# A recurrent block with a mixture of experts: rows split and loaded in another order, the gate's copies on ScalarE, states in a lasting PSUM bank, final sums and reciprocals queued a step later

## The chip, the cores and the metric

The kernel runs on one core of one Trainium2 chip. The metric is the device time of one execution in microseconds (us); several runs give a median. A profile is one execution recorded by the hardware. In it PE is TensorE (PEld its weight loads), DVE is VectorE, ACT is ScalarE, POOL is GpSimd and SP is SyncE, which here issues most of the DMAs. Each engine works through its own queue in order; an instruction that waits holds up all that stand behind it on that engine.

## The reference

There are 8 sequences of 512 tokens with 512 features, 16 heads of 32, and 16 experts of which each token takes 4. All is float32.

```
xn = layernorm(x)                                  # per token, no weights
q, k = rotate(silu(xn @ Wq)), rotate(silu(xn @ Wk)); v = xn @ Wv
o  = lightning_attention(q, k, v)                  # chunks of 128 tokens, a state of 32x32 per head
     # o_chunk = (q k^T * D) v + (q * decay_q) S ;  S = lam^128 * S + (k * decay_k)^T v
o  = o * sigmoid(xn @ Wg1 @ Wg2)                   # the gate
o  = o / sqrt(mean of squares per head + eps) * norm_weight
s  = o @ Wo
p  = softmax(xn @ gate_w.T); top 4, renormed
mixed  = sum over the 4 of p_e * (silu(xn @ Wg[e]) * (xn @ Wu[e])) @ Wd[e]
shared = (silu(xn @ sWg) * (xn @ sWu)) @ sWd * sigmoid(xn @ shared_gate_w)
out = x + s * silu(mixed + shared)
```

## The kernel before

The program has three stages.

The first stage (0 to about 340 us) normalises all eight sequences, routes their tokens, computes the shared expert, and runs the attention of sequences 0 and 1 among it. `norm(b)` makes statistics (DVE, L245 and L247), 1/std (POOL, L249 and L251) and centred rows (DVE, L237) in place in the tile `x_b`; there are three `x` buffers. `halves(b)` splits the low and the high halves of the second 256 features with four POOL copies (L266) and stores them in `xn_d`, from which the experts' rows are gathered later. `turn(b)` transposes the rows on PE (L285) and copies them out on ACT (L287). `load_x(b)` (L147) issues the next rows on SP. `route_1`, `route_2`, `share_1` and `share_2` do the router and the shared expert. The generator `first()` yields these pieces in order, and `along()` inserts them between the pieces of attention: nine fifths of a piece at each step. At the end of the stage, `sort()` and `table()` work out for each of 143 blocks of 128 rows which tokens it holds, with large DVE operations and PE matmuls (L517) in between.

The second stage (about 350 to 785 us) is the 143 expert blocks, each a gather, transposes, two matrix products and a scaled store to `y_d`.

The third stage (about 790 us to the end) runs the attention of sequences 2 to 7 (`sequence`, and `last_sequence` for 7), about 75 us each, with the mixture and the output of all tokens among it. `mixture(b, t)` loads the shared part into `m` (12 buffers), gathers four rows per token on POOL (L1107), adds them on POOL (L1113, L1116) and DVE (L1118, L1121) and applies Silu on ACT (L1124). It is a generator: each call of `advance()` (the `step` of a sequence) takes every active mixture a piece further. `last` multiplies by `s` (DVE, L1135), adds `x` (POOL, L1142, into `xo` with 4 buffers) and stores the result (L1143).

Order on the engines: PE's matmuls are fixed in program order by `on_pe()`. `behind(engine)` does the same for single instructions of POOL, DVE and ACT: they are queued behind the last one traced. All others are placed by a scheduler that may move them within its limits. A PSUM tile comes from `bank(tag, name)`: tag `a` has four banks, `k` and `m` one each, `d` two.

The gate of sequence b: `gate_1` makes `xn @ Wg1` in four row groups (PE, L568) and copies it to SBUF (DVE, L572, tile `g1`); `gate_2` adds the four groups with one matmul (PE, L577, `pf`) and copies that too (DVE, L579, tile `g2`); `gate_3` multiplies by Wg2 (PE, L588, `p`) and takes the sigmoid on ACT (L591, `on`).

The states: `by_token(b, g)` transposes three chunks of keys into bank `k` (PE, L622, `pk`) and scales them out (DVE, L625, `kd`). `scores` then writes the chunks' key-value products into the last 128 columns of the same bank (PE, L640), scores into four `a` banks (PE, L651), and DVE runs the recurrence over the products (L654 and L656, `state`) and masks the scores (L667). `output` adds both parts (PE, L679 and L685). `squares(b)` squares on ACT (L696), sums on PE (L699), takes the root on ACT (L703) and the reciprocal on DVE (L704); `normed(b)` spreads it and multiplies. `project` is the product with Wo (PE, L726).

Of the kernel before, what the change touches and what calls it, by code (L numbers as in the profile page):

```python
# [16 lines left out]
ALU = mybir.AluOpType  # L17
# [77 lines left out]
def tile_block(ctx: ExitStack, tc: tile.TileContext, a: dict, out: bass.AP):  # L95
# [8 lines left out]
    def bank(tag, name):  # L104
        return pp.tile([P, 512], F32, tag=tag, name=name, bufs={"a": 4, "k": 1, "m": 1, "d": 2}[tag])
# [155 lines left out]
    def halves(b):  # L261
        xs = xs_of[b]
        for t in range(NC):
            hs = p1.tile([P, D], U16, tag="hs", name=f"hs_{b}_{t}", bufs=4)
            with behind(POOL):
                nc.gpsimd.tensor_copy(  # L266
                    hs.rearrange("p (h d) -> p h d", h=2),
                    xs[:, t, D // 2 :].bitcast(U16).rearrange("p (d h) -> p h d", h=2))
            g = b * NC + t
            nc.sync.dma_start(xn_d[g * P : (g + 1) * P, D : 2 * D], hs)  # L270
        xs_of.pop(b)

    def turn(b):

# [271 lines left out]

    between = [lambda: None]

    def value(b, t):
        if t == 0:  # L550
            v_of[b] = att.tile([P, NC, D], F32, tag="v", name=f"v_{b}", bufs=2)
        pv = bank("d" if t % 2 else "m", f"pv_{b}_{t}")
        for k in range(KC):
            with on_pe():
                nc.tensor.matmul(  # L555
                    pv, lhsT=xT_of[b][:, k, t * P : (t + 1) * P], rhs=wv[:, k, :],
                    start=(k == 0), stop=(k == KC - 1))
            between[0]()
        nc.scalar.copy(v_of[b][:, t, :], pv)
# [4 lines left out]
    def gate_1(b):  # L564
        pg1 = bank("a", f"pg1_{b}")
        with on_pe():
            for k in range(KC):
                nc.tensor.matmul(  # L568
                    pg1[k * Q : (k + 1) * Q, :], lhsT=wg1[:, k, :], rhs=xT_of[b][:, k, :],
                    start=True, stop=True)  # L570
        g1_of[b] = att.tile([P, N], F32, tag="tmp", name=f"g1_{b}", bufs=TMP)
        nc.vector.tensor_copy(g1_of[b], pg1)  # L572

    def gate_2(b):
        pf = bank("a", f"pf_{b}")
        with on_pe():
            nc.tensor.matmul(pf, lhsT=four, rhs=g1_of[b], start=True, stop=True)  # L577
        g1_of[b] = att.tile([P, N], F32, tag="tmp", name=f"g2_{b}", bufs=TMP)
        nc.vector.tensor_copy(g1_of[b], pf)  # L579

    def gate_3(b):
        on_of[b] = home(b).tile([P, G, N], F32, tag="on", name=f"on_{b}", bufs=1)
# [33 lines left out]

    def by_token(b, g):

        pk = bank("k", f"pk_{b}_{g}")
        with on_pe():  # L620
            for c in range(NC - 1):
                nc.tensor.transpose(  # L622
                    pk[:, c * P : (c + 1) * P], kT_of[g][:, c * C : (c + 1) * C], ident)
        kd = scr[0].tile([P, NC - 1, HG, HD], F32, tag="kd", name=f"kd_{b}_{g}")
        nc.vector.tensor_tensor(  # L625
            kd, pk[:, : (NC - 1) * P].rearrange("p (c h d) -> p c h d", c=NC - 1, d=HD),
            dk[:, g * HG : (g + 1) * HG].unsqueeze(1).unsqueeze(3).to_broadcast(
                [P, NC - 1, HG, HD]), ALU.mult)
        kd_of[g] = pk[:, (NC - 1) * P :], kd
# [62 lines left out]
    def squares(b):  # L692
        pr = bank("a", f"pr_{b}")
        for g in range(G):
            sq = scr[0].tile([P, N], F32, tag="sc", name=f"sq_{b}_{g}", bufs=4)
            nc.scalar.activation(sq, on_of[b][:, g, :], AF.Square)  # L696
            with on_pe():
                for c in range(NC):
                    nc.tensor.matmul(  # L699
                        pr[c * Q : (c + 1) * Q, :C], lhsT=sel[:, H - HG - g * HG :][:, :Q],  # L700
                        rhs=sq[:, c * C : (c + 1) * C], start=(g == 0), stop=(g == G - 1))
        rs = att.tile([P, C], F32, tag="tmp", name=f"rs_{b}", bufs=TMP)
        nc.scalar.activation(rs, pr[:, :C], AF.Sqrt, bias=eps_rms, scale=1.0)  # L703
        nc.vector.reciprocal(rs, rs)  # L704
        rs_of[b] = rs

    def normed(b):
        pbs = [bank("a", f"pb_{b}_{c}") for c in range(NC)]
# [34 lines left out]
    def sequence(b, step, projected, before=None, defer=False, also=lambda: None):  # L743


        n = b + 1

        def project_tiles(q, ts):
            if q is not None:
                for t in ts:  # L750
                    projected(q, t, project(q, t))


        fill = ([0], [1], [2], [3], [], [], [], [])
        for g in range(G):
            scores(b, g)
            step()
            if g + 2 < G:
                key(b, g + 2)
            else:  # L760
                value(n, 2 * (g - 2))
            if g == 0 and b not in on_of:
                gate_3(b)
            if g + 1 < G:
                by_token(b, g + 1)
            project_tiles(before, fill[2 * g])
            step()
            if g + 2 < G:
                query(b, g + 2)
                if g + 3 == G and n not in xT_of:  # L770
                    load_xT(n)
            elif defer:
                (gate_1, gate_2)[g - 2](n)
            if g + 2 == G:
                value(n, 1)
            project_tiles(before, fill[2 * g + 1])
            if fill[2 * g + 1] == [NC - 1]:
                on_of.pop(before, None)
            output(b, g)
            step()  # L780
        v_of.pop(b)
        if n == FIRST:
            gate_1(n)
            squares(b)
            value(n, 3)
            normed(b)
            gate_2(n)
            return
        if defer:
            gate_3(n)  # L790
        value(n, 3)
        also()
        squares(b)
        step()
        key(n, 0)
        also()
        query(n, 0)
        normed(b)
        also()
        step()  # L800
        key(n, 1)
        by_token(n, 0)
        query(n, 1)
        also()
        if not defer:
            for gate, half in ((gate_1, [0, 1]), (gate_2, [2, 3])):
                gate(n)
                project_tiles(b, half)
                also()
            on_of.pop(b)  # L810
        step()

    def last_sequence(b, step, projected, before):
# [44 lines left out]
        for g in range(G):  # L858
            scores(b, g)
            step()  # L860
            if g + 2 < G:
                key(b, g + 2)
            if g > 1:
                project_before(2 * g - 3)
            if g:
                squares_of(g - 1)
            if g + 1 < G:
                by_token(b, g + 1)
            step()
            if g + 2 < G:  # L870
                query(b, g + 2)
            if g in (1, 2):
                project_before(2 * g - 2)
                normed_of(g - 1)
            output(b, g)
            step()
        add_up(0, (0, 1))
        normed_of(G - 2)
        add_up(1, (0, 1))
# [19 lines left out]
    def first():  # L899

        for b in range(B):
            route_1(b)
            yield
            share_1(b)
            yield
            if b + 2 < B:
                norm(b + 2)
            halves(b)
            if b + 3 < B:
                load_x(b + 3)  # L910
            if b + 1 < B:
                turn(b + 1)
                yield
            route_2(b)
            yield
            share_2(b)
            yield
        next(sorting)
# [2 lines left out]
    norm(0)  # L921
    turn(0)
    norm(1)
    pieces = first()
    for _ in range(5):
        next(pieces)
# [120 lines left out]
    def down(i):  # L1047
# [13 lines left out]
            y, py, row(i).bitcast(F32)[:, bass.ds(at, 1)], None, ALU.mult).ins)  # L1061
        nc.sync.dma_start(y_d[i * P : (i + 1) * P, :], y)


    for i in range(4):
        gather(i)
# [64 lines left out]
    def last(b, t, m, s):  # L1131
        xo = comb.tile([P, D], F32, tag="xo", name=f"xo_{b}_{t}", bufs=4)
        nc.sync.dma_start(xo, x[b, t * P : (t + 1) * P, :])
        with behind(DVE):
            nc.vector.tensor_tensor(m, m, s, ALU.mult)  # L1135

        if b + 1 == B and t % 2:
            with behind(DVE):
                nc.vector.tensor_tensor(xo, xo, m, ALU.add)  # L1139
        else:  # L1140
            with behind(POOL):
                nc.gpsimd.tensor_tensor(xo, xo, m, ALU.add)  # L1142
        nc.sync.dma_start(out[b, t * P : (t + 1) * P, :], xo)  # L1143


    m_of, active, steps = {}, [], [0, 0]
    waiting = [(q, t) for q in range(FIRST) for t in range(NC)]
    tiles = []
    for b in range(FIRST, B):
# [4 lines left out]
    def advance():  # L1154

        if steps[1] < len(tiles) and steps[0] * 5 >= steps[1] * 11:
            active.append(mixture(*tiles[steps[1]]))
            steps[1] += 1
        steps[0] += 1
        order = active[:]  # L1160
        while order:
            f = order.pop(0)
# [12 lines left out]
    for b in range(FIRST, B):  # L1175
# [2 lines left out]
            sequence(b, advance, finish, b - 1 if b > FIRST else None, True)  # L1178
        else:
            last_sequence(b, advance, finish, b - 1)  # L1180
    while active or steps[1] < len(tiles):
        advance()
    right.close()
    left.close()
# [53 lines left out]
```

## Time and profile before

| what | value |
|---|---|
| runs | 1246.65, 1247.88, 1249.57 us (median 1247.88) |
| the profiled execution's own time | 1250.12 us |
| its span | 1248.4 us, so 1.7 us lie outside the span |
| PE busy | 1188.4 us, 7799 matmuls and transposes |
| DVE busy | 772.1 us |
| ACT busy | 399.7 us |
| POOL busy | 448.9 us |
| mean granted clock of TensorE | 0.979 |

Busy time is the time in which an engine executes; what is left of the span is idle. The row `PEclk` of the page gives the clock granted to TensorE in tenths of full speed over 40 slices of the span. In a list of waits each line names an engine, the tile and line that waited, what released it, then the sum in us, how many times, and the longest. In a timeline each line has start, duration, engine, line, operation, what it writes and reads, and in brackets the idle time before it and what ended it. A row of the windows view has the window, its length, busy time and count by engine, the granted clock, the DMA share and GB/s.

### The profile page before, as it was taken

The numbers are of one execution on the slowest core, as the hardware profiler recorded it, in microseconds if no ns is written. First come the engines' busy times: TensorE is split into PE (matmuls) and PEld (weight loads), VectorE is DVE, ScalarE is ACT, GpSimd is POOL, SyncE is SP. The second block draws the span as 40 slices with busy tenths as digits, with TensorE's granted clock in tenths as the row PEclk, the third lists the DMA queues.
The fourth block names the chain that finished last, engine by engine and source line by source line (L and its number), as shares of the span: only waits on it lengthen the run. The fifth ranks groups of instructions, "written<-read, shape, count | busy, mean of one in ns | idle before, by whom it ended". The sixth has DMA issues, their size and how long they took to land. (4 is left out here: it accounts for less than half of the span.)

```text
span 1248.4 us, 21569 instructions
## 1 busy us (share of the span) xinstructions
PE 1188.4 (95%) x7799; PEld 703.8 (56%) x7799; DVE 772.1 (62%) x1668; ACT 399.7 (32%) x766; POOL 448.9 (36%) x430
## 2 busy tenths in 40 slices
PE   6988999988989999999999999999999999989997
PEld 3444554445557777777777777444544544445453
DVE  6458745699514444444444344887949879598784
ACT  3333334320144444444444443123141231411420
POOL 2112300300113333333333332580875857858311
PEclk9979899999989999999999999999989999999999
DMA  9676321162248999999999998950844636535112
GB/s 318 212 244 212 144 102 69 42 261 111 100 144 220 229 227 230 221 231 229 226 226 225 227 230 201 320 161 2 287 135 139 224 95 207 175 119 151 43 35 68
DMA packets 167719, 219.77 MB, mean 176 GB/s; under 512 B 93696, under 2 KB 102656, under 8 KB 165696
## 3 DMA queue, kind: packets, MB, share of 16 engines
q1 hardware_dynamic: 145936, 146.17, 40.0%
q0 software_dynamic: 21680, 72.23, 20.9%
q8 instruction: 64, 1.05, 0.3%
q14 instruction: 39, 0.32, 0.1%
HBM read 127.25 MB, written 72.35 MB: 160 GB/s over the span
## 5 line engine op out<-in xcount | busy, mean ns | idle before, releaser
L1030 PE MATMUL pgu<-wexp,xt 128*128 x1144 | 271.7, 381 | 0.7 <-ACT xt L1011 0.4
L1030 PEld LDWEIGHTS pgu<-wexp,xt 128*128 128x128 f32 x1144 | 217.4, 191 | 92.6 <-issue 32.1
L989 POOL DMA_INDIRECT xg<-xn_d,slot x83 | 78.4, 945 | 287.6 <-DVE y L1060 172.0
L1035 DVE TENSOR_TENSOR slb<-slb,pgu 128x128 f32<-128x128 f32 x143 | 41.2, 288 | 205.8 <-ACT slb L1034 205.8
L1013 ACT COPY xt<-pl 128x512 uint16<-128x512 uint16 x143 | 109.6, 767 | 156.3 <-DMA pl<-xg 92.3
L1107 POOL DMA_INDIRECT yg<-y_d,posi x128 | 141.9, 1108 | 49.5 <-DMA m<-sh_d 22.1
L1051 PE MATMUL py<-wexp,hT 128*128 x286 | 147.3, 597 | 0.0
L555 PE MATMUL pv<-wv,xT 128*128 128x512 f32 x256 | 121.3, 612 | 4.9 <-DVE sh L371 3.7
L597 PE MATMUL pk<-xT,wk 128*128 128x512 f32 x256 | 122.9, 621 | 0.0
L597 PE MATMUL pq<-xT,wq 128*128 128x512 f32 x256 | 115.9, 593 | 0.0
L726 PE MATMUL pw<-wo,on 128*128 128x512 f32 x224 | 102.6, 605 | 7.1 <-DVE m L1135 4.2
L1142 POOL TENSOR_TENSOR xo<-xo,m 128x512 f32<-128x512 f32 x30 | 44.6, 1488 | 153.3 <-DVE m L1135 149.3
L989 POOL DMA_INDIRECT more<-xn_d,slot x60 | 56.4, 941 | 114.4 <-DVE y L1060 113.5
L555 PEld LDWEIGHTS pv<-wv,xT 128*128 128x128 f32 x256 | 46.7, 194 | 62.4 <-issue 55.5
L1060 DVE TENSOR_SCALAR y<-py,xg 128x512 f32<-128x512 f32 x83 | 62.3, 750 | 31.4 <-PE py L1051 31.4
L667 DVE TENSOR_TENSOR sc<-ps,dmask 128x512 f32<-128x512 f32 x128 | 79.5, 684 | 0.4 <-PE ps L651 0.4
L597 PEld LDWEIGHTS pq<-xT,wq 128*128 128x128 f32 x256 | 47.3, 191 | 52.2 <-issue 50.9
L597 PEld LDWEIGHTS pk<-xT,wk 128*128 128x128 f32 x256 | 47.5, 196 | 50.2 <-issue 47.7
L726 PEld LDWEIGHTS pw<-wo,on 128*128 128x128 f32 x224 | 41.8, 193 | 58.3 <-issue 46.5
L1034 ACT ACTIVATE slb<-pgu 128x128 f32<-128x128 f32 x143 | 39.7, 278 | 88.7 <-PE pgu L1030 87.5
L602 ACT ACTIVATE sk<-pk 128x512 f32<-128x512 f32 x32 | 19.1, 595 | 122.1 <-PE pk L597 104.1
L1060 DVE TENSOR_SCALAR y<-py,more 128x512 f32<-128x512 f32 x60 | 45.0, 750 | 20.7 <-PE py L1051 20.6
(166 smaller groups left out, 1756.7 us busy)
## 6 DMA issues: line engine op xcount, KB each, us to landing
y_d<-y SPq DMA_DIRECT2D x143, 256.0 KB, 3.1
wexp<-in_experts SPq DMA_DIRECT2D x16, 768.0 KB, 13.0
sh_d<-sh SPq DMA_DIRECT2D x32, 256.0 KB, 2.9
m<-sh_d SPq DMA_DIRECT2D x32, 256.0 KB, 5.4
xo<-in_x SPq DMA_DIRECT2D x32, 256.0 KB, 3.3
out<-xo SPq DMA_DIRECT2D x32, 256.0 KB, 2.0
x<-in_x SPq DMA_DIRECT2D x7, 1024.0 KB, 6.9
xT_d<-xT SPq DMA_DIRECT2D x7, 1024.0 KB, 4.9
```

The lines of the kernel that those rows point to most:

```text
L555: nc.tensor.matmul(pv, lhsT=xT_of[b][:, k, t * P : (t + 1) * P], rhs=wv[:, k, :], start=(k == 0), stop=(k == KC - 1))
L597: nc.tensor.matmul(ps, lhsT=w[:, k, g * P : (g + 1) * P], rhs=xT_of[b][:, k, :], start=(k == 0), stop=(k == KC - 1))
L667: nc.vector.tensor_tensor(s, pss[j].rearrange("p (c t) -> p c t", t=C), dmask[:, g * HG + j].unsqueeze(1).to_broadcast([P, NC, C]), ALU.mult)
L726: nc.tensor.matmul(pw, lhsT=on_of[b][:, g, t * P : (t + 1) * P], rhs=wo[:, g, :], start=(g == 0), stop=(g == G - 1))
L989: nc.gpsimd.indirect_dma_start(out=row(i), out_offset=None, in_=xn_d, in_offset=bass.IndirectOffsetOnAxis(ap=slot[:, i : i + 1], axis=0))
L1013: nc.scalar.copy(xt[:, KP:, :].bitcast(U16).rearrange("p k (t h) -> p h k t", h=2), turned(i).rearrange("p (h k) t -> p h k t", h=2))
L1030: nc.tensor.matmul(pg[:, : 2 * F], lhsT=xt[:, k, :], rhs=wflat[:, bass.ds(off + k * 2 * F, 2 * F)], start=(k == 0), stop=(k == KC - 1))
L1035: nc.vector.tensor_tensor(sl, sl, pg[:, F : 2 * F], ALU.mult)
L1051: nc.tensor.matmul(py, lhsT=hT_of.pop(i), rhs=wflat[:, bass.ds(off_of.pop(i) + KC * 2 * F, D)], start=True, stop=True)
L1060: gone.append(nc.vector.tensor_scalar(y, py, row(i).bitcast(F32)[:, bass.ds(at, 1)], None, ALU.mult).ins)
L1107: nc.gpsimd.indirect_dma_start(out=yg, out_offset=None, in_=y_d, in_offset=bass.IndirectOffsetOnAxis(ap=posi[:, r, g : g + 1], axis=0))
L1142: nc.gpsimd.tensor_tensor(xo, xo, m, ALU.add)
```

## The change

Five things change.

1. In the first stage `halves` and `load_x` move. `halves(0)` and `load_x(3)` come right after `norm(1)`; in iteration b of `first()` it is then `norm(b + 2)`, `halves(b + 1)`, `turn(b + 1)`, `load_x(b + 4)`, where before it was `norm(b + 2)`, `halves(b)`, `load_x(b + 3)`, `turn(b + 1)`. The tile `x_{b+1}` is given up right after its transposes.
2. The gate's two copies out of PSUM go from DVE to ACT.
3. `by_token` takes one tile of bank `k` and keeps it for all sequences (until `kept.clear()`), where before each group took a new tile of the same bank.
4. The reciprocal of `squares` becomes a function `inverse`, called after the next `step()`.
5. The final sum with `x` and its store go into a list `late` and are issued by `advance()` once a full further step has begun, except for the last sequence.

```
@@ halves(b)
-        xs_of.pop(b)
@@ gate_1, gate_2
-        nc.vector.tensor_copy(g1_of[b], pg1)
+        nc.scalar.copy(g1_of[b], pg1)
...
-        nc.vector.tensor_copy(g1_of[b], pf)
+        nc.scalar.copy(g1_of[b], pf)
@@ by_token(b, g)
-        pk = bank("k", f"pk_{b}_{g}")
+        if not kept:
+            kept.append(bank("k", f"pk_{b}_{g}"))
+        pk = kept[0]
@@ squares(b)
-        nc.vector.reciprocal(rs, rs)
         rs_of[b] = rs
+
+    def inverse(b):
+        nc.vector.reciprocal(rs_of[b], rs_of[b])
@@ sequence
         squares(b)
         step()
+        inverse(b)
         key(n, 0)
@@ first
             if b + 2 < B:
                 norm(b + 2)
-            halves(b)
-            if b + 3 < B:
-                load_x(b + 3)
             if b + 1 < B:
+                halves(b + 1)
                 turn(b + 1)
+                xs_of.pop(b + 1)
+                if b + 4 < B:
+                    load_x(b + 4)
                 yield
...
     norm(1)
+    halves(0)
+    xs_of.pop(0)
+    load_x(3)
     pieces = first()
@@ last
+        def add():
+            with behind(POOL):
+                nc.gpsimd.tensor_tensor(xo, xo, m, ALU.add)
+            nc.sync.dma_start(out[b, t * P : (t + 1) * P, :], xo)
+
         if b + 1 == B and t % 2:
             with behind(DVE):
                 nc.vector.tensor_tensor(xo, xo, m, ALU.add)
+            nc.sync.dma_start(out[b, t * P : (t + 1) * P, :], xo)
+        elif b + 1 == B:
+            add()
         else:
-            with behind(POOL):
-                nc.gpsimd.tensor_tensor(xo, xo, m, ALU.add)
-        nc.sync.dma_start(out[b, t * P : (t + 1) * P, :], xo)
+            late.append((steps[0], add))
@@ advance
         steps[0] += 1
+        while late and late[0][0] + 1 < steps[0]:
+            late.pop(0)[1]()
```

More of the change, by code (lines that the diff above doesn't have):

```diff
@@ L547, in tile_block @@
     between = [lambda: None]
+    kept = []
     def value(b, t):
@@ L794, in sequence @@
         step()
+        inverse(b)
         key(n, 0)
@@ L876, in last_sequence @@
             step()
+        kept.clear()
         add_up(0, (0, 1))
@@ L1062, in down @@
         nc.sync.dma_start(y_d[i * P : (i + 1) * P, :], y)
+    kept.clear()
     for i in range(4):
@@ L1139, in last @@
                 nc.vector.tensor_tensor(xo, xo, m, ALU.add)
-        else:
-            with behind(POOL):
-                nc.gpsimd.tensor_tensor(xo, xo, m, ALU.add)
-        nc.sync.dma_start(out[b, t * P : (t + 1) * P, :], xo)
-    m_of, active, steps = {}, [], [0, 0]
+            nc.sync.dma_start(out[b, t * P : (t + 1) * P, :], xo)
+        elif b + 1 == B:
+            add()
+        else:
+            late.append((steps[0], add))
+    m_of, active, late, steps = {}, [], [], [0, 0]
     waiting = [(q, t) for q in range(FIRST) for t in range(NC)]
@@ L1180, in tile_block @@
             last_sequence(b, advance, finish, b - 1)
-    while active or steps[1] < len(tiles):
+    while active or late or steps[1] < len(tiles):
         advance()
```

## The prediction

> **What bounds the kernel now.** I read the page first: its busy rows, and the row of the granted clock.
>
> ```profile
> span 1248.4 us, 21569 instructions
> PE 1188.4 (95%) x7799; PEld 703.8 (56%) x7799; DVE 772.1 (62%) x1668; ACT 399.7 (32%) x766; POOL 448.9 (36%) x430
> PE   6988999988989999999999999999999999989997
> PEclk9979899999989999999999999999989999999999
> ```
>
> TensorE is busy for 95% of the span, so time can go in three ways only: fewer matmuls (the change removes none, and leaves their order alone but for trivia), less of the 60 us (1248.4 - 1188.4) in which PE is idle, or less of the time in which it runs at a reduced clock. The chain of waits names one 0.1% DVE step and helps no further. So I list what ended PE's idle times:
>
> ```profile
> PE pn L517 <- DVE sc L667: 6.7, 3, 3.3
> PE p L588 <- DVE g L579: 5.8, 5, 2.9
> PE pf L577 <- issue: 4.6, 1, 4.6
> PE pk L622 <- DVE state L656: 4.4, 3, 1.7
> PE pw L726 <- DVE m L1135: 4.2, 3, 2.5
> PE ps L651 <- ACT sh L373: 2.7, 1, 2.7
> PE pk L640 <- DVE kd L625: 0.7, 1, 0.7
> ```
>
> The gate's two copies (L572, L579) stand in front of two of the largest. The timeline of the worst of them, sequence 0's gate in the first stage:
>
> ```profile
> 63.92 0.40 SPq L147 DMA_DIRECT2D x<-in_x  x1
> 71.16 0.69 DVE L245 BATCH_NORM_STATS2 st<-x 128x6 f32<-128x512 f32 x1 [3.42 <-DMA x<-in_x]
> 71.77 0.67 DVE L572 COPY g<-pg 128x512 f32<-128x512 f32 x1
> 72.54 2.04 PE L577 MATMUL pf<-g,four 128*128 128x512 f32 x2 [4.61 <-issue]
> 74.62 0.69 DVE L579 COPY g<-pf 128x512 f32<-128x512 f32 x1 [0.92 <-PE pf L577]
> 75.37 2.09 PE L588 MATMUL p<-g,wg 32*128 32x512 f32 x8 [0.78 <-DVE g L579]
> ```
>
> The rows `x` of sequence 4 are asked for at 63.92. DVE, in order, stops on their statistics until 71.16, and the gate's copy behind them has to wait although its input was ready at 67.9. The wait has a second price, in the windows view (busy by engine, then the clock):
>
> ```profile
> 0.00:70.00 70.00, 57.62 (x192) 26.99 (x192) 36.20 (x115) 25.29 (x36) 13.40 (x26) 1.00 0.78 262
> 70.00:87.00 17.00, 13.01 (x39) 7.83 (x40) 10.38 (x39) 7.29 (x12) 4.08 (x6) 0.50 0.67 223
> ```
>
> From 70 to 87 us PE has half its clock. The same happens at 916.3-923.2, after this:
>
> ```profile
> 913.77 0.63 ACT L1124 ACTIVATE m<-m 128x512 f32<-128x512 f32 x1 [1.85 <-DVE m L1121]
> 915.92 0.69 DVE L1118 TENSOR_TENSOR m<-m,yg 128x512 f32<-128x512 f32 x1 [2.19 <-POOL yg L1113]
> 916.53 0.68 DVE L579 COPY g<-pf 128x512 f32<-128x512 f32 x1
> 917.27 2.09 PE L588 MATMUL p<-g,wg 32*128 32x512 f32 x8 [2.95 <-DVE g L579]
> ```
>
> pf was ready at 912.5, but its copy stood behind a mixture sum that waited for POOL.
>
> **The change part by part.**
>
> *Gate passage of sequence 0.* SP now issues x_4 as soon as `halves(1)` and `turn(1)` have used x_1, at about 41 us by the times at which these stand in the trace, not at 63.9; a landing takes 5.3 us (median of the x loads), so the statistics wait for nothing. The copies are on ACT as well: a 128x512 PSUM copy there is 582 to 597 ns (L896, L559, L287) against 683 and 686 on DVE, about 0.7 with the handover. New stalls: pf 0.7, p 0.7, then psT about 0.7, since the sigmoid table load (1.283 us) now stands between the second copy and the sigmoids, where before it lay at 64.16 under matmuls; p's own 1.1 us covers most of it. Before: 4.61 + 0.78 + 0.67 = 6.06. After: 2.1. **-3.9.** Moved with it: five x loads in all, of which the last (x_7) still comes late, at about 103 instead of 115.9, for statistics due at about 108; that is just enough. The waits of L245 for x (12.9 us on DVE) go.
>
> *Clock at 70-87.* At half clock pf, p, psT, pl and pk took 2.04 + 2.09 + 3.68 + 1.73 + 5.61 = 15.15 us; the same shapes elsewhere take 1.06, 1.14, 1.91, 0.96 and 3.60, sum 8.67. If no gap is longer than 0.7 us the clock should stay: **-6.5.** [...] By the trace, idle gaps of 1.85 us (366.4), 2.73 (121.5) and 2.95 (917.3) halved it too, while 3.06 (30.7) and 2.50 (1034.1) did not; and recovery took 14.5 us of broken work here, 6 at 917. [...] I go by the rows. [...] transposes between 35 and 60 us ran at 1.00.
>
> *Rows split earlier.* `halves(0)` moves on POOL from behind rstd_2 (23.97) to behind rstd_1 (15.88), beside DVE's L237 at 16.96. There four L237 took 1.92 us alone, and 3.06 at 24.04 with the hs copies beside them: +1.1 on the DVE chain up to sh L371, which PE awaits at 30.74 (3.06 idle, no slack). **+1.1.** SP issues the xn_d stores earlier; DMA has room (share 0.00 at 50-60 us).
>
> *Table stretch, 250-330.* DVE is busy 70.1 of 80 us and PE waits for it (pn 6.7): two DVE copies of 0.69 fewer, **-1.4.** After it, gate 1's copy now stands on ACT between two squares and waits for its matmul: **+0.6** on that chain (one copy).
>
> *Gate in the last stage.* For sequences 5 and 6 (stalls 0.96 at 1077.6 and 0.86 at 1158.3) the copy follows the v copy on ACT, which is idle: -1.8. At 917 it follows the Silu of 913.77 and can end at about 915.0, so that the stall is 0.8, not 2.95: -2.15. At 838 (0.25) I change nothing. **-4.0.** With it the clock at 916.3-923.2: p 2.09 for 1.14 and pv 5.69 for 3.70: **-3.0.** What is queued behind the copy on ACT: the squares (they have over a step of matmuls as cover) and the next Silu of a mixture.
>
> *Final sums and reciprocals.* POOL waited 149.3 us for DVE's m L1135 in front of L1142 (1.49 us each), with the gathers queued behind. Now the sum comes at least one step later, behind gathers that need not wait, and its out DMA later on SP. DVE waited 32.7 us over 7 for the root at L704; now a mixture sum (0.9 to 1.0 us) comes first, and key plus query (7.2 us of PE) still cover the reciprocal. PE's share in all this is bounded by what it waits for from DVE's queue in that stage: pk 4.4 + pw 4.2 + kd 0.7 = 9.3. A full removal is -9.3; a loss would be a sum that holds one of 12 m or 4 xo buffers too long, up to one such wait (2.5) per sequence. These PE waits also end on DVE's own sums, which are as many as before; DVE gets 0.69 us fewer twice in each 75 us. I take **-2**.
>
> *Lasting bank.* The transposes L622 wait for the state operations L656, which read the same bank: that is data, and reusing the tile does not take it away. Only PE's wait on its own L640 goes: **0**, bounded by pk's 4.4.
>
> Sum: -3.9 - 6.5 + 1.1 - 1.4 + 0.6 - 4.0 - 3.0 - 2.0 = -19.1. Against the profiled execution's own 1250.1: 1231.0. That one is 2.2 above the median of the runs (1247.88), so **1229**.
>
> **The rivals.**
>
> *The clock does not follow* (gaps of 0.7 in a row, PE half idle for 4 us, then transposes; at 917 another gap of near 2). For it: 1.85 was enough at 366. Against: the gates at 838 and 1077 kept 1.00 with gaps of 0.25 and 0.96. Clock terms gone: -9.6, **1238**.
>
> *Larger.* Relief of POOL and DVE removes all 9.3 (7.3 more), and x_6 in time takes DVE's 2.65 wait at 106.2 out of the chain to lg and sh, so that the ps stall at 121.5 (2.73) goes, and its half clock to 131 (pg 6.14 for 3.70): 5.1 more. Against: PE arrives about 9 us sooner there, and DVE is busy 25 of 33 us. All of it 1217; half **1223** to it.
>
> *Slower, by ACT's order.* ACT waits 76.8 us over 22 (mean 3.5, longest 7.8) for DVE's L1121 in front of mixture Silus. A gate copy queued behind such a Silu waits as well, and PE's p or pf with it. It does so for sequences 2, 3 and 4 at least. With 3.5 each and 3 of half clock, in all six sequences, that is +39; in three, +19.5, in place of -9.0 for the last stage: 1250.1 - 9.3 - 0.8 + 19.5 - 2.2 = **1257**. It decides once the Silu's input comes over 2 us later than the DVE copy would have been done; at 917 it came 2.8 before.
>
> *Given back.* PE reaches the ps stall of 121.5 about 9 us sooner, and DVE, whose chain sets its end, was idle for only 14.6 us of 70-120 (6.6 and 8.0 by the windows), part of it in front of POOL. If its chain sets that time, most of the first stage's 9.3 returns there, and the last stage's 9.0 likewise in waits on DVE's other results: about **1246**. Against: the x waits (3.42, 2.47, 2.65) are part of that idle time and go.
>
> **How the numbers follow.** My forecast 0.47; clock does not follow 0.23; larger 0.15; ACT's order 0.09; given back 0.06. The first three, and a little of the last, lie below 1245.4: faster 0.86, within 0.2% (2.5 us, about what a measurement of this kernel can tell from no change) 0.05, slower 0.09. The range reaches down to the larger case in full, less 3 for one of the two dips of the clock in the table stretch (268-271, 288-291, after pn waits of 3.34 and 2.12), and up to partial cases at 1244.
>
> **What would show it.** Right: in PE's waits no pf over 1 us near 70; p under 1 each; clock 1.00 over 65-87 and at 916; L245 no longer waits for x; pk from state still about 4. Wrong: 0.50 at 70-87 without a long gap (rival 1); p or pf waiting for ACT g over 2 us behind L1124's successor (rival 3); PE waiting for xT or m with SP held by late out stores.

## The result, and the profile after

The changed kernel takes 1229.58 us (median of 6 runs, 1226.41 to 1232.70) against 1247.47 us for the kernel before in the same comparison (median of 6, 1246.52 to 1249.57). The ratio is 0.9855, with a 95% interval of 0.9835 to 0.9875. The profiled execution took 1229.70 us. The lines of the kernel after are shifted by -1 to +14 (L285 is L284, L577 is L578, L656 is L659, L1135 is L1149).

The page of the kernel after, its first rows and those of PE and its clock in 40 slices:

```profile
span 1227.9 us, 21563 instructions
PE 1177.3 (96%) x7799; PEld 696.7 (57%) x7799; DVE 768.2 (63%) x1652; ACT 407.3 (33%) x782; POOL 448.5 (37%) x430
PE   6998999989999999999999999999999999999997
PEclk9998999999999999999999999999999999999999
```

The span is 20.5 us shorter. PE does the same 7799 instructions in 11.1 us less busy time (1188.4 to 1177.3). That goes with the clock, which stood at half for 52.0 us of the span before and for 22.7 us after; its mean rose from 0.979 to 0.991. The other 9.4 us is idle time (60.0 to 50.6).

What ended PE's idle times in the kernel after (sum in us, times, longest):

```profile
PE pn L516 <- DVE sc L670: 6.4, 3, 4.3
PE pk L625 <- DVE state L659: 4.1, 4, 1.6
PE ps L654 <- DVE sh L370: 3.4, 1, 3.4
PE pk L643 <- DVE kd L628: 3.0, 2, 2.3
PE p L589 <- ACT g L580: 1.0, 3, 0.7
PE pf L578 <- ACT g L573: 0.7, 1, 0.7
PE pw L731 <- DVE m L1149: 0.6, 1, 0.6
```

The 4.6 us of pf and the 5.8 of p are down to 0.7 and 1.0; pw from m is down from 4.2 to 0.6; kd is up from 0.7 to 3.0; pk from the states is where it was. The gate of sequence 0, in the timeline of the kernel after:

```profile
69.56 0.59 ACT L573 COPY g<-pg 128x512 f32<-128x512 f32 x1 [3.28 <-PE pg L569]
70.20 1.12 PE L578 MATMUL pf<-g,four 128*128 128x512 f32 x2 [0.71 <-ACT g L573]
71.36 0.59 ACT L580 COPY g<-pf 128x512 f32<-128x512 f32 x1 [1.22 <-PE pf L578]
72.00 1.14 PE L589 MATMUL p<-g,wg 32*128 32x512 f32 x8 [0.68 <-ACT g L580]
73.91 2.12 PE L284 MATMUL psT<-ident,x 128*128 128x128 f32 x16 [0.77 <-ACT on L592]
```

and the clock over it (windows view, the clock behind PE, PEld, DVE, ACT and POOL):

```profile
70.00:77.00 7.00, 5.36 (x35) 3.43 (x36) 2.13 (x5) 5.76 (x11) 1.36 (x3) 1.00 1.01 370
```

Three gaps of about 0.7 us stand where gaps of 4.61, 0.78 and 0.67 stood, and the clock stays at 1.00.

**Marks.** The same matmuls stand in both traces, so the distance between two of them can be compared. I use five stretches: A, from the router product of sequence 2 (plT, 58.81 before) to that of sequence 4 (116.95), which holds the gate of sequence 0; B, from there to the transposes of sequence 5 (135.90), which holds the ps stall near 121; C, from pf of sequence 2 (337.69) to the first expert block (357.61); D, from pf of sequence 4 (911.40) to the squares' sums of sequence 3 (924.91), the place of the 2.95 us wait; E, from there to the spread of sequence 6 (1171.2). All in us, each from one profile:

| kernel | A | B | A+B | C | D | E |
|---|---|---|---|---|---|---|
| before | 58.14 | 18.95 | 77.09 | 19.92 | 13.51 | 246.3 |
| after | 48.30 | 16.54 | 64.84 | 16.33 | 7.45 | 246.5 |
| after_again | 48.30 | 17.03 | 65.33 | 17.25 | 7.45 | 255.2 |
| after_third | 48.30 | 16.97 | 65.27 | 17.30 | 7.46 | 246.3 |
| gate_rows | 48.29 | 17.01 | 65.30 | 17.34 | 8.53 | 253.5 |
| a_gate_dve | 55.18 | 15.36 | 70.54 | 17.47 | 7.45 | 254.9 |
| b_rows | 55.19 | 15.39 | 70.58 | 17.66 | 8.58 | 255.1 |
| b_gate | 53.12 | 24.58 | 77.70 | 19.17 | 8.52 | 253.8 |
| b_bank | 57.84 | 18.89 | 76.73 | 16.94 | 8.59 | 253.6 |
| b_late | 57.92 | 19.15 | 77.07 | 17.26 | 7.46 | 254.5 |
| b_fill | 64.03 | 17.34 | 81.37 | 17.16 | 8.58 | 252.2 |
| a_no_late | 48.30 | 16.45 | 64.75 | 17.36 | 8.23 | 246.3 |
| a_no_inv | 48.30 | 16.58 | 64.88 | 19.77 | 7.87 | 246.1 |
| best_7h | 48.30 | 11.25 | 59.55 | 17.30 | 7.45 | 246.3 |

The stretches account for the two profiled executions: 1.6 us more ahead of A, then -9.8, -2.4, -3.6, -6.1 and +0.2 from A to E, and -0.3 in all that lies between, make 20.4 of the 20.5 us.

In two of the three comparisons below (the one of b_gate to b_late, and the one of after_again to b_fill) all kernels, those with the old code too, take 6 to 9 us more in E, and 2 to 14 more between the first expert block and D. PE's idle time there ends on `issue`, on nothing that the profile shows: rows such as `pk <- issue`, 2.3 to 3.7 us in b_bank, b_gate and b_rows, which the profiles of before, of after and of the last comparison do not list. Times are therefore compared only with the kernel before of the same comparison. A ratio is the one on record; it need not be the quotient of the two medians beside it.

### The profile page after: what moved, and what is told of

It reads as the page before. It is cut to its first block, busy times and chain, and to the rows that moved or that the text cites. A ratio compares the mean times of both kernels' runs of the same rounds, so it can differ in the third digit from the quotient of the medians.

```text
span 1227.9 us, 21563 instructions
## 1 busy us (share of the span) xinstructions
PE 1177.3 (96%) x7799; PEld 696.7 (57%) x7799; DVE 768.2 (63%) x1652; ACT 407.3 (33%) x782; POOL 448.5 (37%) x430
## 5 line engine op out<-in xcount | busy, mean ns | idle before, releaser
L556 PEld LDWEIGHTS pv<-wv,xT 128*128 128x128 f32 x256 | 46.4, 193 | 60.9 <-issue 55.2
L603 ACT ACTIVATE sk<-pk 128x512 f32<-128x512 f32 x32 | 19.1, 597 | 117.5 <-PE pk L598 102.1
```

The lines of the kernel that those rows point to most:

```text
L556: nc.tensor.matmul(pv, lhsT=xT_of[b][:, k, t * P : (t + 1) * P], rhs=wv[:, k, :], start=(k == 0), stop=(k == KC - 1))
```

## The experiments

### One part alone, four times

**b_gate**, the copies alone:

```
-        nc.vector.tensor_copy(g1_of[b], pg1)
+        nc.scalar.copy(g1_of[b], pg1)
...
-        nc.vector.tensor_copy(g1_of[b], pf)
+        nc.scalar.copy(g1_of[b], pf)
```

> The kernel before with only the gate's two copies on ACT. My theory (either part alone frees the gate in the first stage, since the copy no longer stands behind statistics that wait for x_4; and only the copies free it in the last stage): the pf wait of 4.6 us near 72 falls under 1, the clock stays at 1.00 over 70-87, the p wait of 2.95 near 917 falls under 1 with full clock after it; about 14 us faster (10 in the first stage, 4 to 6 in the last), 1232 to 1235. The rival (the two parts add up, because x_4 still comes at 71 and DVE's later results are late for PE): no more than 8 us faster, 1239 to 1242, with a new PE wait on DVE between 72 and 125.

Measured: 1264.65 against 1262.28 us, ratio 1.001 (0.9986 to 1.0035). My theory missed by 14 us. The gate itself went as I expected (stretch A is 5.0 shorter), and B then took it all back and more, 24.58 against 18.95. Two rows of the DVE timeline of b_gate:

```profile
105.83 0.69 DVE L245 BATCH_NORM_STATS2 st<-x 128x6 f32<-128x512 f32 x1 [2.76 <-DMA x<-in_x]
120.21 1.29 DVE L245 BATCH_NORM_STATS2 st<-x 128x6 f32<-128x512 f32 x2 [1.31 <-DMA x<-in_x]
```

and its PE timeline over B:

```profile
116.45 0.40 PE L640 MATMUL pk<-v,kd 128*32 128x32 f32 x24 [3.28 <-DVE kd L625]
119.99 2.07 PE L651 MATMUL ps<-qT,kT 32*128 32x128 f32 x12 [2.51 <-ACT sh L373]
125.29 2.67 PE L651 MATMUL ps<-qT,kT 32*128 32x128 f32 x16 [3.23 <-DVE sh L371]
```

PE comes sooner, DVE does not: its statistics still wait for rows that SP asks for as late as before (18.6 us of such waits, 12.9 in the profile of before), so PE waits 9.0 us (3.28 + 2.51 + 3.23) for kd and sh where before it waited 3.3 (2.73 + 0.57).

**b_rows**, the order of splitting and loading alone:

```
+    halves(0); xs_of.pop(0); load_x(3)          # behind norm(1)
...
-            halves(b)                           # which also gave x_b up
-            if b + 3 < B: load_x(b + 3)
             if b + 1 < B:
+                halves(b + 1)
                 turn(b + 1)
+                xs_of.pop(b + 1)
+                if b + 4 < B: load_x(b + 4)
```

> The kernel before with only the new order of splitting and loading rows in the first stage. My theory: the gate's copy, still on DVE, no longer stands behind statistics that wait, so the passage near 72 goes as in the changed kernel (about 9 to 10 us) and the ps stall's half clock near 121 shrinks (about 2); the last stage keeps its 2.95 us wait near 917. About 1236, 11 us faster. The rival (the copies on ACT are what freed the gate): the passage near 72 keeps most of its wait and half clock, and the time is within 4 us of before.

Measured: 1251.82 against 1262.28 us, ratio 0.9915 (0.9886 to 0.9944): near the theory in time, not in its working. Stretch A is only 3.0 shorter and B 3.6. The timeline of b_rows shows what is left of the pf wait:

```profile
68.35 0.81 DVE L237 TENSOR_SCALAR x<-x,mv,rstd 128x512 f32<-128x512 f32 x1 [1.48 <-POOL rstd L251]
69.08 0.67 DVE L355 TENSOR_TENSOR h<-sl,pu 128x512 f32<-128x512 f32 x1
69.68 0.79 DVE L237 TENSOR_SCALAR x<-x,mv,rstd 128x512 f32<-128x512 f32 x1
70.39 0.67 DVE L570 COPY g<-pg 128x512 f32<-128x512 f32 x1
71.12 1.84 PE L575 MATMUL pf<-g,four 128*128 128x512 f32 x2 [2.04 <-DVE g L570]
73.79 2.09 PE L586 MATMUL p<-g,wg 32*128 32x512 f32 x8 [0.83 <-issue]
```

The statistics there no longer wait for the DMA, but the copy now stands behind POOL's 1/std and behind h and the centring of rows. Behind this gap of 2.04 us PE is slow again: pf takes 1.84 us and p 2.09, 1.12 and 1.14 in the kernel after.

**b_bank**, the lasting bank alone (`kept` in `by_token`, cleared before the bank's other users):

> The kernel before with only the lasting bank for pk. My theory: the transposes still wait for the state operations, so PE's pk wait on DVE state stays between 4 and 5 us and the time is the same within 2.5 us. The rival (the new tile's release was what PE waited for): the pk wait goes, and the time falls by 4 us or more.

Measured: 1262.14 against 1262.28 us, ratio 0.9995 (0.9978 to 1.0012). PE's wait is still there (2.3 us in this execution, 4.1 in the kernel after, 4.4 before; below my 4 to 5 here, but 2.6 in b_rows without the bank):

```profile
PE pk L626 <- DVE state L660: 2.3, 3, 1.5
```

The bank does nothing that can be measured, as the data dependence says.

**b_late**, the later sums and reciprocals alone (`late` in `last` and `advance`, `inverse` in `sequence`):

> The kernel before with only the later final sums and the later reciprocals. My theory from the changed kernel's trace, where POOL still waits 137 us for the products in front of its sums (149 before): no change within 2.5 us. The rival (POOL and DVE are relieved and PE's waits in the last stage shrink): 3 us or more faster, pw and pk waits of the last stage under half of before.

Measured: 1258.85 against 1262.28 us, ratio 0.998 (0.9958 to 1.0003). The interval includes 1, and the medians are 3.4 us apart, a little more than I named. What I had not expected is that PE's wait for m fell to 0.6 us; kd rose to 2.5.

### The parts together

**gate_rows** is before with the two first-stage parts only; **a_gate_dve** is after with the copies back on DVE (`nc.vector.tensor_copy`); **after_again** is the changed kernel beside them.

> The changed kernel once more, beside the two below. If the first stage's gain doesn't depend on the chip, its ratio to before is again near 0.986 (0.984 to 0.989). If the split into single parts (1.001 for the gate's copies alone, 0.9915 for the rows alone) were all there is, and the parts simply added, it would be 0.990 or more.

> The kernel before with the gate's copies on ACT and the new order of rows together, and nothing else. My theory (the two need each other: with the copies alone the statistics still wait for x_4 and the time comes back as waits for DVE near 121; with the rows alone the copy still stands in DVE's queue): the marks of the first stage move as in the changed kernel, about 10 us by 135, and the time is that of the changed kernel within 3 us. The rival (parts add): 5 us or less by 135, ratio 0.990 or more.

> The changed kernel with the gate's two copies back on DVE. My theory: as the rows alone, about 2 us of pf wait near 70, half clock behind it, first stage 5 us and not 10 ahead of before; 5 to 8 us slower than the changed kernel, ratio to before about 0.991. The rival (late sums and reciprocals free DVE's queue, so that the copy's place no longer matters): within 3 us of the changed kernel.

Measured, against 1258.53 us: after_again 1240.80 (0.9876, 0.9843 to 0.9910), gate_rows 1246.18 (0.9899, 0.9867 to 0.9931), a_gate_dve 1248.84 (0.9916, 0.9888 to 0.9945). In stretch A+B, relative to the 77.09 of before: copies alone +0.6, rows alone -6.5, both -11.8 in gate_rows, -11.8 to -12.3 in three profiles of the kernel after, and -6.6 again when the copies go back to DVE. So the two parts do need each other, and the first stage's gain is theirs: adding the single parts would give -5.9. In time, gate_rows is 5.4 us behind after_again, not within the 3 I expected; their intervals overlap, and stretch D shows 1.1 of it (8.53 against 7.45). In the two profiles 5.5 us more lie between the last expert block and pf of sequence 3 (60.6 us in gate_rows, 55.1 in after_again), where gate_rows has more of PE's waits that end on `issue` (4.3 us behind 790, 2.0 in after_again). That stretch follows none of the edits: it takes 54.5 us in b_fill, which has none of the five parts, 55.2 in b_bank and 61.2 in b_late.

**b_fill**, the wait without the idle time:

```
+        if b == 0:
+            pz = bank("a", "pz")
+            with on_pe():
+                for _ in range(9):
+                    nc.tensor.matmul(pz, lhsT=wv[:, 0, :P], rhs=wv[:, 0, :], start=True, stop=True)
         g1_of[b] = att.tile([P, N], F32, tag="tmp", name=f"g1_{b}", bufs=TMP)
```

> The kernel before, and in the gate of sequence 0 nine more 128x512 matmuls into a spare bank behind the gate's first product, whose result is not used; they occupy PE while the copy waits. It separates the wait from the clock. If the idle gap is what halves the clock, it stays at 1.00 over 70-87 and the transposes of sequence 4's router product (plT) come about 6 us earlier although the copy is no sooner; near 121 the time comes back as waits for DVE, as it did with the copies alone, so the whole is within 4 us of before. If the short matmuls and transposes behind the gap keep the clock low by themselves, it is 0.50 there as before and nothing moves.

Measured: 1257.93 against 1258.53 us, ratio 1.0009 (0.999 to 1.0028). The filler was 8 us long, about twice what I had meant, so plT came later (A is 64.03), not 6 us earlier. For the clock it still tells something. The PE timeline of b_fill:

```profile
66.34 7.99 PE L576 MATMUL pz<-wv 128*128 128x512 f32 x18
78.34 1.28 PE L595 MATMUL p<-g,wg 32*128 32x512 f32 x8 [3.14 <-DVE g L586]
```

and its windows view:

```profile
66.00:79.00 13.00, 9.86 (x32) 4.03 (x28) 7.29 (x15) 0.00 (x0) 4.09 (x6) 1.00 0.68 245
79.00:89.00 10.00, 9.35 (x37) 6.68 (x30) 3.05 (x13) 4.57 (x10) 0.07 (x1) 0.51 0.78 277
```

With the filler in PE's queue the clock is 1.00 (66 to 79 us); it is halved at about 79.2 (0.51 over 79 to 89), 0.9 us after the end of the next real gap (3.14 us, before p). In this run the clock followed the gap, not the short matmuls.

### Sums or reciprocals, and the next stall

**a_no_late** and **a_no_inv** each put one of the two back in the changed kernel; after_third is their standard.

> The changed kernel again, as the standard for the three below on the same chip: ratio to before 0.985 to 0.989.

> The changed kernel with the final sums and stores back at their old place; the reciprocal stays later. In the four kernels with both edits PE waits for the product m (pw from DVE m) 0.6 or 0.7 us, in the six without them 4.2 to 5.0. If it is the sums, which kept POOL waiting in front of a mixture's gathers and adds, the wait is 4.9 again here, DVE's wait for yg sums is 5 us or more, and the kernel is 2 to 5 us slower than the changed one. If it is the reciprocal, the wait stays 0.6 and the time is the same.

> The changed kernel with the reciprocal back inside squares; the sums stay later. The mirror of the run before: if the sums are the cause, the pw wait stays 0.6 and the time is within 2.5 us of the changed kernel, with DVE's wait for the root at the reciprocal up from 25 to 30 to 33 to 36; if it is the reciprocal, the pw wait is 4.9.

Measured, against 1250.26 us: after_third 1228.95 (0.9844, 0.9806 to 0.9883), a_no_late 1232.30 (0.9858, 0.9821 to 0.9895), a_no_inv 1231.10 (0.9846, 0.9811 to 0.9881). The waits of a_no_late:

```profile
PE pw L730 <- DVE m L1147: 4.4, 3, 2.6
DVE m L1130 <- POOL yg L1125: 19.2, 10, 4.1
DVE m L1133 <- POOL yg L1128: 12.6, 6, 3.4
```

its timeline at the longest of pw's waits:

```profile
1011.23 0.69 DVE L1130 TENSOR_TENSOR m<-m,yg 128x512 f32<-128x512 f32 x1 [2.28 <-POOL yg L1125]
1016.59 1.22 PE L730 MATMUL pw<-wo,on 128*128 128x512 f32 x1 [2.56 <-DVE m L1147]
```

and the waits of a_no_inv:

```profile
PE pw L728 <- DVE m L1143: 0.6, 1, 0.6
DVE m L1129 <- POOL yg L1124: 0.5, 1, 0.5
```

It is the sums: with them at their old place POOL's sum of gathered rows comes late, DVE's mixture sum waits 2.28 us for it, and the product m behind it in DVE's queue frees PE's bank 2.56 us late. What counts is the wait in front of that product, not the sum of such waits: b_gate, b_rows and gate_rows, with the old sums, have only 8 us of DVE's waits for yg, and their pw wait is 4.9 us. Of the 3.8 us of pw wait, the last stage keeps little: from the last expert block to the spread of sequence 6 the marks are only 1.0 us closer in after_third than in a_no_late, since kd takes 2.6 of it back (3.0 against 0.4). The median of a_no_late is 3.4 us behind that of after_third, with overlapping intervals. The reciprocal's move is worth nothing that shows in time: with it at its old place DVE waits 33.7 us for the root, 24.9 in after_third, and PE does not notice.

**best_7h** goes after the stall that is left near 114:

```
-            return behind(engine) if b < 2 else nullcontext()
+            return behind(engine) if b in (0, 1, 7) else nullcontext()
...
     norm(1)
-    halves(0); xs_of.pop(0); load_x(3)
...
+            if b == 0:                            # in first(), behind norm(2)
+                halves(0); xs_of.pop(0); load_x(3)
```

> The changed kernel with two edits in the first stage: the split of sequence 0's rows goes back behind the normalisation of sequence 2, and sequence 7's normalisation is tied to its place in the program, so that its statistics no longer stand in DVE's queue in front of sequence 3's shared outputs while x_7 lands. My theory of the second stall (ps waits 3.4 us near 114 for DVE sh, behind a 1.6 us wait for x_7 and 1.3 us of statistics; half clock for 7 us after it): the wait falls under 1 us, the clock stays, and the transposes of sequence 5 come 4 to 6 us earlier than in the changed kernel; the first edit gives about 1 us by the router product of sequence 1. Together 4 to 6 us faster than the changed kernel, ratio to before about 0.983. The rival (the stall near 114 is the router's long DVE chain itself): the marks at 135 stay within 1.5 us and the time within 2.5 us.

Measured: 1224.87 us (1223.24 to 1228.45) beside 1228.95 (1227.39 to 1236.40) for the changed kernel; ratio to before 0.9805 (0.977 to 0.9841). The timeline of the kernel after, with sequence 7's statistics in front of sequence 3's sh:

```profile
109.09 1.29 DVE L245 BATCH_NORM_STATS2 st<-x 128x6 f32<-128x512 f32 x2 [1.61 <-DMA x<-in_x]
113.37 0.74 DVE L370 TENSOR_SCALAR sh<-pys,sg 128x512 f32<-128x512 f32 x1
114.17 2.67 PE L654 MATMUL ps<-qT,kT 32*128 32x128 f32 x20 [3.38 <-DVE sh L370]
```

its windows view:

```profile
112.00:120.00 8.00, 5.83 (x24) 3.88 (x25) 7.18 (x18) 0.00 (x0) 0.08 (x1) 0.57 0.22 85
```

and both views of best_7h at the same place:

```profile
108.00 0.74 DVE L370 TENSOR_SCALAR sh<-pys,sg 128x512 f32<-128x512 f32 x1
109.99 1.15 PE L654 MATMUL ps<-qT,kT 32*128 32x128 f32 x14 [0.27 <-DVE lT L301]
```

```profile
108.00:117.00 9.00, 8.63 (x54) 4.97 (x47) 5.01 (x11) 0.60 (x1) 0.00 (x0) 1.00 0.42 164
```

The stall and the half clock are gone and B is 11.25 for 16.97: 5.7 us shorter, the theory's 4 to 6. The median is 4.1 us lower; the intervals of the two ratios overlap, so the stretch shows this more surely than the time does. Its other edit, the split put back, gave nothing: the router product of sequence 1 stands at 34.07 against 33.27 in after_third.

## Why the prediction was right, point by point

The number fits (1229 forecast, 1229.58 measured), and the largest step is right with its mechanism; several of the smaller ones are not, and their errors cancelled. That the number fits to 1 us is luck: 7.0 of the 19.1 us were forecast for the gate in the last stage, where the change gives nothing that shows. Stretch B, which the sum had at nothing, and a rest that is not placed (below) took their room.

- **Gate passage and its clock**: forecast -3.9 - 6.5 = -10.4, stretch A -9.84 in the profile after, and 48.30 in every kernel that has both parts. x_4 was asked for at 42.27 (forecast about 41). The landing of 5.3 us is a misreading: it is the median of eleven loads, four of them of a quarter of the size, and the seven whole ones take 6.9 us (median); here that changed nothing. What the step did not say is that neither edit is enough alone. The expectations of b_gate and b_rows took either as enough, and these runs show that each leaves half of the cause.
- **x_7, "just enough"**: wrong. It was asked for at 102.0 (forecast about 103), but its statistics still waited 1.6 us, and PE's stall of 3.4 us and the half clock from 113 stand behind them. best_7h, where these statistics no longer stand in front, shows what that was worth: 5.7 us.
- **Given back near 121** (a rival at 0.06): in the kernel after it did not happen, B is 2.4 shorter. In b_gate it happened in full. What I named against this rival, that the waits for x go, is what makes the difference (18.6 us of them in b_gate, 5.8 in gate_rows).
- **Rows split earlier, +1.1**: wrong. In the kernel after L237 takes 3.06 us at 16.05 and 1.92 at 25.04; before it was 1.92 and then 3.06. The slow pass changed places, it was not added, and PE's wait for sh, which was to grow by 1.1, fell from 3.06 to 1.92. What the profile after does have there is a half clock at 31-34.5, behind a gap of 1.92 us; after_third has a gap of 1.94 us there and keeps the clock.
- **Table stretch and squares, -1.4 and +0.6**: measured 0.0 (229.4 to 335.5 before, both ends 10.8 earlier after). The first pn wait grew (3.34 to 4.26) and the two copies fewer bought nothing.
- **Gate in the last stage, -4.0, and its clock, -3.0**: the step that failed. D is 6.1 shorter in the kernel after, but it is 7.45 in a_gate_dve and 7.46 in b_late too, with both copies on DVE, and 8.5 to 8.6 in b_bank, b_rows and b_fill, with copies on DVE and the old sums. So the wait of 2.95 us and the half clock of 916-923, about 5.0 of the 6.1, belong to that one execution of before, as far as these kernels tell (all of them ran in the two comparisons with the longer E). The later sums and reciprocals are worth the other 1.1, and ACT nothing. At sequences 5 and 6 p's waits did go (0.96 and 0.86 before, none after, 0.64 and 1.15 in a_gate_dve), but the -1.8 did not come in time: E is 246.3 before and 246.5 after, 254.9 in a_gate_dve and 255.2 in after_again. In the kernel after, kd waits (0.7 to 3.0, one of them 2.3 with 3.7 us of matmuls taking 5.4 behind it) took their place.
- **Sums and reciprocals, -2 of at most 9.3**: about -1.1, by D and by a_no_late. pw's 4.2 went as the upper bound had it, kd gave most of it back.
- **Lasting bank, 0**: right.
- **Not in the sum**: C is 3.6 shorter after. But it is 16.9 to 17.7 in b_bank, b_late, b_fill and b_rows as well, and 19.77 in a_no_inv: again executions, not the change.
- **Gaps and the clock**: the gaps that the forecast went by left open which of them halves the clock, and the last section shows that the length alone does not tell. Behind 2.04 us of idle time pf and p took 1.84 and 2.09 us (b_rows); behind 1.92 us it was half clock from 31.0 to 34.4 (the kernel after). Behind the three gaps of 0.7 us in the kernel after the clock was 1.00 (70 to 77 us), over the 16 transposes too.

What stays open: the first stage gives 11.8 to 12.3 us and the sums about 1, but the medians differ by 17.9, so about 5 us are not placed. In the two profiles the places for it are C and D, and there kernels with the old code also ran without the loss. The clock does not place it: in the last comparison the runs of before have a median granted clock of 0.982, those of after_third 0.991, and 0.009 of 1250 us is 11 us. Of these, 10.2 are accounted for by A and B, by an estimate from the profiles of before and after (27.3 us at half clock there before, 6.8 after). Nor does such a rest need any of the edits: b_fill takes as long as before although its A+B is 4.3 us longer, and behind the first stage its code is that of before. Where the runs of before spend these 5 us is not shown.

## What to carry to other kernels

A copy that unblocks the critical engine should stand on a queue where nothing ahead of it waits for a DMA or another engine; and when the critical engine is then freed, look at once at what the blocked queue still delivers late, because the time comes back there unless its own wait is taken away too. A gap before PE can cost more in clock than in waiting (in the profile of before, behind 4.61 us of waiting, matmuls took 15.15 us at half clock that take 8.67 elsewhere), so the worth of a removed wait is to be read with the clock behind it. Before a stall is put into a forecast, ask if it belongs to the program's order or to one execution: the stall of 2.95 us at 917 stands in one profile only, and no other kernel with that code has more than 1.0 us there.

## What the runs showed of the hardware

In these runs the length of a gap does not tell by itself if the clock is halved. Four profiles have PE idle before sequence 0's v product. Its row in the kernel after, in a_no_inv, in after_third and in before:

```profile
30.60 5.40 PE L556 MATMUL pv<-wv,xT 128*128 128x512 f32 x8 [1.92 <-DVE sh L370]
```

```profile
30.74 5.40 PE L555 MATMUL pv<-wv,xT 128*128 128x512 f32 x8 [1.92 <-DVE sh L369]
```

```profile
29.64 3.70 PE L556 MATMUL pv<-wv,xT 128*128 128x512 f32 x8 [1.94 <-DVE sh L370]
```

```profile
30.74 3.70 PE L555 MATMUL pv<-wv,xT 128*128 128x512 f32 x8 [3.06 <-DVE sh L371]
```

and the windows view of the kernel after over the time at half clock:

```profile
31.01:34.42 3.41, 3.41 (x5) 1.35 (x4) 0.53 (x3) 0.00 (x0) 0.00 (x0) 0.50 1.07 368
```

Behind 1.92 us of idle time the clock fell at 31 us in the kernel after and in a_no_inv. Behind 1.94 us it stayed at 1.00 in after_third, which is the same kernel as after, and behind 3.06 us it stayed at 1.00 in before. What else decides it these rows do not show.

So a gap of 1.9 us is punished in one execution and not in the next. At 31 us it costs about 1.7 us (eight matmuls in 5.40 for 3.70), which would be a part of the spread between runs of one kernel: the six runs of the changed kernel go from 1226.41 at clock 0.994 to 1232.70 at 0.987.
